# Four more third joins, six paired summing steps and a tenth read buffer in a one-core graph-network kernel

## The chip, the core and the metric

The kernel runs on one core of a Trainium2 chip. The metric is the device time of one execution in microseconds (us). Five engines work side by side: TensorE (PE; its weight loads are shown as PEld), VectorE (DVE), ScalarE (ACT), GpSimd (POOL) and SyncE (SP), which here only issues DMAs. They wait for each other through semaphores.

## What is computed

A graph layer over 6250 nodes and 206250 edges, padded to 1612 tiles of 128 edges:

```
msg  = concat(x[dst], edge_attr)             # per edge
h    = relu(msg @ W1a.T + b1a) @ W1b.T + b1b # per edge
agg  = segment_sum(h, src) / max(count, 1)   # per node
z    = relu(concat(x, agg) @ W2a.T + b2a) @ W2b.T + b2b
out  = layernorm(x + concat(z, x) @ Wr.T + br)
```

The second layer's weights are applied after the sum over the edges, so that only the first layer's rows, 128 wide, have to be summed per node. The edges come in the order of `dst`; the sum goes by `src`. The rows are therefore sorted through memory.

## The kernel before, in words

**Blocks.** The edges are taken in 124 blocks of 13 tiles. The loop runs `for k, ep_ in enumerate(epoch_of)`; PE, DVE, ACT and SP run in exactly the order in which the program is written (a manual schedule), GpSimd's queue holds the scatters.

**First layer and scatter.** For a block, `hidden` (matmuls at L1461, eviction with Relu by ACT at L1465) makes the first-layer rows of each tile in a row buffer `orow`; there are four (`ROWS`), so block k needs the buffer that block k-4 has scattered. `scatter` then sends each tile's 128 rows to their slots in the table `rows` in memory by one indirect DMA of GpSimd (L1513). The slots are sorted by `bin` = src // 128, of which there are 49. `scatter(k - LEAD)` is called two blocks behind.

**Joins.** In blocks 2 to 109 part of a block goes another way. A join takes three tiles and gathers edges of the same bin into quads of four rows. It costs marks (DVE at L1302, ACT at L1314 and L1318), six matmuls with the marks (L1348), a copy by ACT (L1353), eight matmuls for the rows (L1363) with two evictions (L1366), and one indirect DMA that scatters all quads (L1485). `joined(k)` says how many joins block k has: three in the blocks of the tuple `THRICE`, otherwise two. A block with j joins has 13 - 3j tiles that go directly, and so 13 - 2j scatters. The scatters of a block wait for places in the next block's work on PE (`pace`).

**Sums.** The rows of one bin are summed per node by one matmul for each tile of 128 slots (L1647, two matmuls each in the trace) against a one-hot matrix that DVE makes (L1627). The tiles come from memory by DMAs of SP (`read`, L1593) into the `READS` buffers `rt`. Low slots of a bin are full long before all edges are there: `FULL` lists, for each epoch, how many tiles a bin has when a step ends; `FULLQ` does so for the quads' slots. A step's reads wait until the scatters of the last blocks that may write there have landed. The first steps of both lists are paired: a group reads both steps' tiles of up to three bins, with at most 12 tiles (`SUMS, TILES = 3, 12`). A planner opens each pair three blocks (`LATE`) after its tiles are full, and gives each block as many tiles as `RATES[joined(k)]` allows. `sum_first`, `sum_rest` and `sum_next` do the sums; `collect` adds them to `part` (DVE at L1718; the first sum of a bin is copied by ACT). What is left when the joins end (10 tiles a bin) is summed from block 113 on. The blocks are three epochs of 110, 12 and 2 blocks with tables of their own: the second epoch's 162 tiles can be read when block 121 has been scattered, the last epoch's 51 when block 123 has.

**Other work in the loop.** Every second block from 10 to 58 computes two bins' share of the second layer ahead of time (`nodes_at`). `clear` has SP write zeros into slots that no edge may fill. `bins` splits src into bin and place (a few instructions of DVE and ACT) for blocks further on; src lies in memory that the read buffers `rt` use later (`lent`), so it has to be done before the first read.

**The end.** After the loop the last groups go through a pipeline of stages: means, product (POOL at L2056), transpose, second layer, residual, norm, store.

Of the kernel before, what the change touches and what calls it, by code (L numbers as in the profile page):

```python
# [453 lines left out]
NEAR = 8  # L454
HEAD = 117
NEXT = 468
FULL = ((3, 6, 9, 12), (1,), ())
BIG = 2.0**20
LATE = 3
RD = 6  # L460
SUMS, TILES = 3, 12
SEG = 9
PRE, AHEAD_FROM, EVERY = 9, 10, 2
RATES = {0: 55, 2: 18, 3: 10}
RING = 8
ROWS, EDGES, READS = 4, 4, 9
SPREAD = 4.8
EARLY = 30
CLEAR = 12
LEAD = 2  # L470
JOIN, QUAD, MARKS = 3, 4, 3
JOIN_FROM, JOIN_TO = 2, 110
THRICE = (*range(9, 27, 2), *range(34, 99, 8))
JOINS = 3 if THRICE else 2
PACED = range(PRE, 123)
SIDES, ENATS, CHUNK = 2, 2, 2
ON_ACT = 1
FULLQ = (3, 6, 9, 11, 13)
NODES = 8
FIRST = 4  # L480

# [8 lines left out]
def fast_path(  # L490
# [39 lines left out]
    NT = srcT.shape[1]  # L530
    E = NT * P
    NB = N // P + 1
# [22 lines left out]
    def joined(k):  # L555
        if not JOIN_FROM <= k < JOIN_TO:
            return 0
        return 3 if k in THRICE else 2

# [6 lines left out]
    def by_bin(of_bin, of_rest):  # L566
        return [of_bin] * (NB - 1) + [of_rest]
# [9 lines left out]
    def low_of(b, n, first=0):  # L577
        _, mean, dev = edges_of(b, n, first)
        return max(0, int(mean - dev)) // P
# [9 lines left out]
    def quads_low(b, n):  # L589
        _, mean, dev = quads_of(b, n)  # L590
        return max(0, int(mean - dev)) * QUAD // P
# [10 lines left out]
    for e, n in enumerate(EPOCHS):  # L602
# [15 lines left out]
        ep_.steps, lo = [], by_bin(0, 0)  # L618
        for t in FULL[e]:
            at = next(k for k in range(n) if low_of(0, k, ep_.first) >= t)  # L620
# [24 lines left out]
    qep.steps, lo = [], by_bin(0, 0)  # L645
    for t in FULLQ:
        at = next(k for k in range(qep.end + 1) if quads_low(0, k) >= t)
# [129 lines left out]
    with (  # L777
# [253 lines left out]

        NBAD = 15 + 5 * NE + 2 * sum(map(len, FULL)) + 2 * len(FULLQ)
        bad = const.tile([P, NBAD], F32, name="bad")
# [527 lines left out]
        def clear(e, i):  # L1561

            ep_ = epochs[e] if e else shared
            v = rows_of(ep_)
            step = (NB - 1) // CLEAR
            parts = [(i * step, (i + 1) * step)] + [(NB - 1, NB)] * (i == CLEAR - 1)
            for b0, b1 in parts:
                lo, hi_ = ep_.low[b0], max(ep_.top[b0:b1])
                if e:
                    lo, hi_ = ep_.stride // P - hi_, ep_.stride // P - lo  # L1570
                for l in range(lo, hi_, PADT):
                    c = min(l + PADT, hi_)
                    s = nc.sync.dma_start(
                        v[b0:b1, l * P : c * P, :].rearrange("b (p r) f -> p b (r f)", p=P),
                        padrow[:, None, : (c - l) * W].to_broadcast([P, b1 - b0, (c - l) * W]),
                    )
                    if e == 0:
                        for group_ in ("qslots", "slots0"):
                            tc.declare_no_dep(s.ins, group=group_, reason="no edge has these slots yet")
                        tc.add_to_no_dep_group("cleared", s.ins)  # L1580
                        cleared.append(s.ins)
# [71 lines left out]
        def groups_of(stage):  # L1653


            def size(b):
                return sum(st.hi[b] - st.lo[b] for st in stage)

            runs = []
            for b in range(NB):  # L1660
                if size(b) == 0:
                    continue
                if not runs or len(runs[-1]) == SUMS or sum(map(size, runs[-1])) + size(b) > TILES:
                    runs.append([])
                runs[-1].append(b)
            res = []
            for run in runs:
                reads = []
                for st in stage:
                    i = 0  # L1670
                    while i < len(run):
                        lo, hi_ = st.lo[run[i]], st.hi[run[i]]
                        nb, c = 1, hi_ - lo
                        while (
                            i + nb < len(run) and (st.lo[run[i + nb]], st.hi[run[i + nb]]) == (lo, hi_)
                            and (nb + 1) * c <= RD
                        ):
                            nb += 1
                        reads += [(st, run[i], nb, t0, n) for t0, n in tiles_of(lo, hi_)]
                        i += nb  # L1680
                res.append(reads)
            return res
# [69 lines left out]
        def tiles_in(groups):  # L1752
            return sum(nb * n for g in groups for _, _, nb, _, n in g)

        groups_at, queue, credit = [[] for _ in range(NGR + 1)], [], 0
        early_on = epochs[0].full
        assert len(early_on) <= len(qep.full)
# [6 lines left out]
        for k in range(NGR + 1):  # L1764
            for stage, at in zip(summing, open_at):
                if k == at:
                    queue += groups_of(stage)
            if k == NGR:
                groups_at[k] = queue
                break  # L1770
            until = min(o for o in opens if o > k)
            credit += min(RATES[joined(k)], max(tiles_in(queue) - credit, 0) / (until - k))
            while queue and credit > 0:
                groups_at[k].append(queue.pop(0))
                credit -= tiles_in(groups_at[k][-1:])
            credit = min(credit, 0)
        to_issue = []

        def issue(k):

            while to_issue and sum(len(g.reads) for g in issued + marked + halves) + len(to_issue[0]) <= READS:
                issued.append(Sums(k, to_issue.pop(0)))
# [17 lines left out]
        def nodes_cols(b0):  # L1800
            n = min(CHUNK, NB - b0)
            return n, slice(b0 * P, (b0 + n) * P)

        def nodes_load(b0):
            n, cols = nodes_cols(b0)
            have = min(N, cols.stop) - cols.start
            if have < n * P:
                nc.vector.memset(top.xin[:D, have : n * P], 0.0)
            nc.sync.dma_start(top.xin[:D, :have], xT[:, cols.start : cols.start + have])
# [18 lines left out]
                xrs[:, b0 : b0 + n, :], top.nx[:, n * P : n * (P + D)].rearrange("p (b f) -> p b f", f=D)  # L1828
            )

        nodes_at = {AHEAD_FROM + EVERY * i: b0 for i, b0 in enumerate(range(0, NB, CHUNK))}
        assert JOIN_FROM - 3 < AHEAD_FROM - 1 and max(nodes_at) < JOIN_TO

        bins_at = {NEAR - 2: (HEAD, NEXT), 22: (NEXT, 754), 24: (754, 1040), 26: (1040, 1326), 28: (1326, NT)}
        range_at = {4: (0, ALU.min), 5: (1, ALU.max)}
        assert NEXT % (SEG * BLK) == 0 and NEXT // BLK > max(bins_at) + 3
        for g in range(3):
# [9 lines left out]
        for k, ep_ in enumerate(epoch_of):  # L1847
# [71 lines left out]
            if k in range_at:  # L1919
                i, o = range_at[k]  # L1920
# [50 lines left out]
                nodes_store(nodes_at[k - 1])  # L1971
            if k + 1 in nodes_at:
                nodes_load(nodes_at[k + 1])
            if k in clears:
                clear(*clears[k])
            issue(k)

            if not joined(k):
                g = sum_first(k) if due > 0 else None
# [250 lines left out]
```

## Time and profile before

| | us |
|---|---|
| median of 3 runs | 1533.61 (1531.03 to 1533.70) |
| profiled execution | 1534.22 |
| its span, first to last instruction | 1532.4 |
| PE busy | 1440.7 (94%) |
| DVE busy | 1341.7 (88%) |
| POOL busy | 1128.8 (74%) |
| ACT busy | 1114.6 (73%) |

Mean granted TensorE clock over the span: 0.983. A busy share is a mean over stages with different limits; times on PE are modelled, so neighbouring matmuls overlap and the mean duration of one is longer than the distance between two starts. In rows of groups the numbers behind the bar are busy us, mean ns of one, and the engine's idle us before them with what ended it. In rows of the timeline stand the start, the length, engine, line, what is written and read, and in brackets the idle time before it. A row of a window has, for each engine, its busy us and its instructions in brackets; then the granted TensorE clock, the DMA share and GB/s.

### The profile page before, as it was taken

To read this page: it belongs to the slowest core of one execution; us is meant where nothing else is said; L and a number is where in the kernel's file an instruction comes from. 1 tells how busy PE (TensorE), PEld (TensorE's weight loads), DVE (VectorE), ACT (ScalarE), POOL (GpSimd) and SP (SyncE) were. 2 spreads that over 40 slices of the span, in tenths; PEclk is the share of its full clock that TensorE was granted. 3 is DMA by queue.
4 is the path that set the end of the run, shared out by engine and by line. 5 is a ranking of instruction groups with operands and counts; after the bars stand their busy time and mean duration, and the time that the engine had idled before them with its cause. 6 is when DMAs were issued, how large, how long until landed. Compare 5 with 4: busy or idle time off the path is not lost.

```text
span 1532.4 us, 33764 instructions
## 1 busy us (share of the span) xinstructions
PE 1440.7 (94%) x11008; PEld 1274.8 (83%) x11008; DVE 1341.7 (88%) x2882; ACT 1114.6 (73%) x2413; POOL 1128.8 (74%) x1198
## 2 busy tenths in 40 slices
PE   5989999987999999999989998999999999999997
PEld 4767777766888988888878888989888899999896
DVE  8789999887898988979889898999999988788787
ACT  3689999996898888878878887887887744332004
POOL 6777777777777777777777777777777777777734
PEclk9899999998999999999999999999999999999999
DMA  8798998967788888777877767777677899999884
GB/s 206 221 301 284 302 303 288 308 188 257 238 262 256 251 253 270 221 229 224 231 238 214 233 213 244 237 227 250 210 242 229 279 322 320 345 343 310 264 275 115
DMA packets 255427, 390.92 MB, mean 255 GB/s; under 512 B 43412, under 2 KB 186838, under 8 KB 255242
## 3 DMA queue, kind: packets, MB, share of 16 engines
q1 hardware_dynamic: 206874, 265.50, 58.7%
q0 software_dynamic: 47840, 122.94, 22.8%
q8 instruction: 90, 1.47, 0.4%
q14 instruction: 95, 0.78, 0.2%
q10 hardware_dynamic: 528, 0.22, 0.1%
HBM read 213.72 MB, written 174.78 MB: 254 GB/s over the span
## 4 chain that ended last, share of the span: by engine, by line
PE 57%; DMA 16%; ACT 11%; DVE 7%; issue 5%; POOL 2%; SPq 1%; DVEq 0%; ACTq 0%; POOLq 0%
PE place L1647 22%; PE place L1348 11%; DMA rows<-orow,rowidx 9%; PE place L1461 9%; PE place L1363 8%; DMA rt<-rows 3%; DMA rows<-orow,qidx 3%; ACT orow L1366 2%; ACT marks L1314 2%; ACT marks L1318 1%; DVE marks L1302 1%; POOL rows L1513 1%; DVE oh L1627 1%; ACT orow L1465 1%; ACT rhs L1414 1%
## 5 line engine op out<-in xcount | busy, mean ns | idle before, releaser
L1513 POOL DMA_INDIRECT rows<-orow,rowidx x910 | 878.3, 965 | 288.0 <-issue 142.5
L1647 PE MATMUL place<-rt,oh 128*128 128x129 f32 x3952 | 483.7, 277 | 15.3 <-ACT orow L1366 5.9
L1647 PEld LDWEIGHTS place<-rt,oh 128*128 128x128 f32 x3952 | 467.7, 193 | 27.2 <-DVE oh L1627 8.3
L1627 DVE TENSOR_TENSOR oh<-ramp,rt 128x768 f32<-128x768 bf16 (+4 forms) x391 | 309.6, 824 | 42.4 <-DMA rt<-rows 41.3
L1465 ACT ACTIVATE orow<-place 128x512 f32<-128x512 f32 (+2 forms) x263 | 142.5, 542 | 224.5 <-PE place L1461 219.3
L1485 POOL DMA_INDIRECT rows<-orow,qidx x234 | 226.1, 966 | 71.3 <-issue 19.8
L1302 DVE TENSOR_TENSOR marks<-quad_ramp,ramp 128x1024 fp32r<-128x1024 f32 x234 | 273.4, 1213 | 1.5 <-ACT z_act L1310 1.5
L1363 PE MATMUL place<-mv,rj 128*128 128x130 f32 x1872 | 242.7, 280 | 33.9 <-ACT orow L1465 20.6
L1348 PE MATMUL place<-marks,side 128*128 128x512 f32 x702 | 267.5, 410 | 0.0
L1461 PE MATMUL place<-mv,rhs 124*128 124x128 f32 x1820 | 262.5, 289 | 4.7 <-ACT orow L1465 3.8
L1363 PEld LDWEIGHTS place<-mv,rj 128*128 128x128 f32 x1872 | 223.1, 192 | 44.5 <-ACT orow L1465 24.5
L1348 PE MATMUL place<-marks,rest 128*64 128x512 f32 x702 | 240.2, 396 | 0.0
L1461 PEld LDWEIGHTS place<-mv,rhs 124*128 124x128 f32 x1820 | 229.6, 197 | 6.2 <-ACT orow L1465 4.0
L1348 PEld LDWEIGHTS place<-marks,side 128*128 128x128 f32 x702 | 134.3, 191 | 51.6 <-issue 2.0
L1366 ACT ACTIVATE orow<-place 128x260 f32<-128x260 f32 x468 | 163.7, 389 | 13.4 <-PE place L1363 4.1
L1314 ACT ACTIVATE marks<-quad_ramp,z_act 128x512 fp32r<-128x512 f32 x234 | 168.9, 722 | 6.1 <-PE place L1348 2.7
L1318 ACT ACTIVATE marks<-marks,ones 128x512 fp32r<-128x512 f32 x234 | 169.8, 725 | 4.1
L1121 DVE TENSOR_TENSOR_SCAN had<-ramp,bins 128x400 bf16<-128x400 bf16 (+2 forms) x124 | 127.2, 1026 | 13.7 <-ACT orow L1452 1.7
L1353 ACT COPY rj<-place 128x512 f32<-128x512 f32 x234 | 133.3, 570 | 1.9 <-PE place L1348 1.9
L1348 PEld LDWEIGHTS place<-marks,rest 128*64 128x64 f32 x702 | 96.0, 137 | 38.6 <-issue 0.8
L1414 ACT ACTIVATE rhs<-rhs,ones 60x896 f32<-60x896 f32 (+2 forms) x116 | 123.7, 1066 | 3.7
L1412 ACT ACTIVATE rhs<-rhs,from_win 60x896 f32<-60x896 bf16 (+2 forms) x116 | 123.6, 1065 | 2.9
(197 smaller groups left out, 1594.7 us busy)
## 6 DMA issues: line engine op xcount, KB each, us to landing
rt<-rows SPq DMA_DIRECT2D x194, 390.0 KB
rt<-rows SPq DMA_DIRECT2D x97, 325.0 KB
rows<-padrow SPq DMA_DIRECT2D x24, 1040.0 KB
rhs<-in_edgeT SPq DMA_DIRECT2D x90, 224.0 KB
enat<-in_edgeJ SPq DMA_DIRECT2D x90, 192.0 KB
rows<-orow,rowidx POOLq DMA_INDIRECT x910
rt<-rows SPq DMA_DIRECT2D x40, 260.0 KB
rt<-rows SPq DMA_DIRECT2D x48, 195.0 KB
```

The lines of the kernel that those rows point to most:

```text
L1302: nc.vector.tensor_tensor(m[:, :n, :], all_q[:, None, :].to_broadcast([P, n, QUAD * P]), z[:, :n, None].to_broadcast([P, n, QUAD * P]), op ...
L1314: nc.scalar.activation(m[:, t, :], all_q, AF.Square, bias=z_acts[k][:, i * JOIN + t : i * JOIN + t + 1], scale=-1.0)
L1318: nc.scalar.activation(m[:, t, :], m[:, t, :], AF.Relu, bias=ones[:, :1], scale=-1.0)
L1348: done[k, f"turn{i}"] = nc.tensor.matmul(ps[: w.shape[1], :], w, m[:, t, :], start=t + p == 0, stop=last and p == 1).ins.name
L1363: done[k, f"join{i}"] = nc.tensor.matmul(ps[:, j, :], rj[:, (g0 + j) * P : (g0 + j + 1) * P], m, start=True, stop=True).ins.name
L1366: nc.scalar.activation(mrow[:, g0 : g0 + 2, :], ps, AF.Relu)
L1461: done[k, c] = nc.tensor.matmul(ps[:, j, :], rhs[:WIDE, of * P : (of + 1) * P], m[:WIDE, :H], start=True, stop=True).ins.name
L1465: nc.scalar.activation(orow_of(k, k0, n)[:, :, :H], ps[:, :n, :], AF.Relu)
L1485: s = nc.gpsimd.indirect_dma_start(out=qep.rows.rearrange("(q r) f -> q (r f)", r=QUAD), out_offset=bass.IndirectOffsetOnAxis(ap=qidx[:, q ...
L1513: s = nc.gpsimd.indirect_dma_start(out=ep_.rows, out_offset=bass.IndirectOffsetOnAxis(ap=rowidx[:, k % RING * BLK + j : k % RING * BLK + j ...
L1627: nc.vector.tensor_tensor(res[:, at_tile : at_tile + nb * n, :], ramp[:, None, :].to_broadcast([P, nb * n, P]), node[:, :, None].to_broadc ...
L1647: m = nc.tensor.matmul(of_bin(b), oh[:, at, :], rows, start=i == 0, stop=i == len(of) - 1)
```

## The change

- `THRICE`: the blocks with three joins are, beside 9 to 25 in steps of 2, now 34 to 106 in steps of 6 (13 blocks) and no more 34 to 98 in steps of 8 (9 blocks): 22 for 18. There are 238 joins for 234.
- `FULL[0]` and `FULLQ` have six steps for four and five, all paired: 5, 4, 4, 4, 3 and 4 tiles a bin, where there were 6, 6, 6 and 5 tiles and a step of 2 tiles for the quads alone. A group can then hold three bins and not two. The first pair opens at block 28 (33 before). 11 tiles a bin stay for block 113 and later (10 before).
- `RATES[2]`: up to 14 tiles in a block with two joins (18 before), and `LESS`: 4 fewer in the blocks of `nodes_at`.
- `READS`: ten read buffers for nine.
- `bins_at`: the last four pieces of `bins` two blocks earlier.
- `issue(k)`, which issues reads, is called ahead of `clear` in a block.

```diff
-FULL = ((3, 6, 9, 12), (1,), ())
+FULL = ((2, 4, 6, 8, 9, 11), (1,), ())
...
-RATES = {0: 55, 2: 18, 3: 10}
+RATES = {0: 55, 2: 14, 3: 10}
+LESS = 4
 RING = 8
-ROWS, EDGES, READS = 4, 4, 9
+ROWS, EDGES, READS = 4, 4, 10
...
-THRICE = (*range(9, 27, 2), *range(34, 99, 8))
+THRICE = (*range(9, 27, 2), *range(34, 107, 6))
...
-FULLQ = (3, 6, 9, 11, 13)
+FULLQ = (3, 5, 7, 9, 11, 13)
...
+        nodes_at = {AHEAD_FROM + EVERY * i: b0 for i, b0 in enumerate(range(0, NB, CHUNK))}
...
-            credit += min(RATES[joined(k)], max(tiles_in(queue) - credit, 0) / (until - k))
+            credit += min(RATES[joined(k)] - LESS * (k in nodes_at), max(tiles_in(queue) - credit, 0) / (until - k))
...
-        nodes_at = {AHEAD_FROM + EVERY * i: b0 for i, b0 in enumerate(range(0, NB, CHUNK))}
...
-        bins_at = {NEAR - 2: (HEAD, NEXT), 22: (NEXT, 754), 24: (754, 1040), 26: (1040, 1326), 28: (1326, NT)}
+        bins_at = {NEAR - 2: (HEAD, NEXT), 20: (NEXT, 754), 22: (754, 1040), 24: (1040, 1326), 26: (1326, NT)}
...
                 nodes_load(nodes_at[k + 1])
+            issue(k)
             if k in clears:
                 clear(*clears[k])
-            issue(k)
```

## The prediction, written before the changed kernel ran

> **What bounds the kernel now.** I read the page first, then the windows, then GpSimd's timeline, last the chain and SP's waits around the end.
>
> ```profile
> span 1532.4 us, 33764 instructions
> PE 1440.7 (94%) x11008; PEld 1274.8 (83%) x11008; DVE 1341.7 (88%) x2882; ACT 1114.6 (73%) x2413; POOL 1128.8 (74%) x1198
> L1513 POOL DMA_INDIRECT rows<-orow,rowidx x910 | 878.3, 965 | 288.0 <-issue 142.5
> L1485 POOL DMA_INDIRECT rows<-orow,qidx x234 | 226.1, 966 | 71.3 <-issue 19.8
> ```
>
> By shares PE looks like the bound and POOL looks a quarter idle. Windows of single stages and POOL's own timeline say otherwise:
>
> ```profile
> 130.00:330.00 200.00, 190.68 (x1295) 152.48 (x1293) 186.39 (x436) 193.84 (x431) 151.39 (x158) 0.99 0.90 287
> 330.00:930.00 600.00, 564.78 (x4272) 496.89 (x4271) 520.73 (x1092) 503.26 (x1072) 456.40 (x472) 0.98 0.77 235
> 930.00:1230.00 300.00, 294.03 (x2332) 264.82 (x2331) 279.89 (x568) 241.06 (x495) 227.74 (x238) 1.00 0.77 242
> 1230.00:1400.00 170.00, 168.06 (x1485) 165.82 (x1484) 141.48 (x271) 64.06 (x86) 129.13 (x135) 1.00 1.03 334
> ...
> 77.63 0.96 POOL L1513 DMA_INDIRECT rows<-orow,rowidx  x1 [1.51 <-ACT orow L1366]
> 91.48 0.96 POOL L1513 DMA_INDIRECT rows<-orow,rowidx  x1 [2.54 <-ACT orow L1366]
> 262.53 0.96 POOL L1513 DMA_INDIRECT rows<-orow,rowidx  x1 [1.05 <-DMA rows<-orow,rowidx]
> ...
> 1380.08 0.96 POOL L1513 DMA_INDIRECT rows<-orow,rowidx  x1 [0.30 <-issue]
> 1381.34 0.95 POOL L1513 DMA_INDIRECT rows<-orow,rowidx  x1 [0.30 <-issue]
> ...
> 1467.27 0.96 POOL L1513 DMA_INDIRECT rows<-orow,rowidx  x1 [0.30 <-issue]
> ```
>
> In each window row the fifth busy time is POOL's, with its scatters in brackets: 158 in 200 us, 472 in 600, 238 in 300, 135 in 170. That is one per 1.26 to 1.27 us whatever PE does. The timeline shows why: 0.96 us busy, then 0.30 us that no wait explains, so starts lie 1.26 us apart (1380.08, 1381.34). After 20 us only three gaps are longer, 4.2 us together beyond their 0.30. So the 1144 scatters are one unbroken stream that ends at 1467.27 + 0.96 = 1468.23, and the "idle" 26% of POOL is a gap that comes with every scatter. POOL is the pacemaker of the blocks.
>
> PE runs ahead of it. The first block of 13 scatters, block 110, begins on PE at 1220.66 (first row below). On POOL 182 scatters remain from there: 1468.23 - 182 x 1.264 = 1238.2. The lead is 17.5 us. Four row buffers limit it: in the second row PE stands 4.20 us because a row buffer is not yet free.
>
> ```profile
> 1220.66 2.40 PE L1461 MATMUL place<-mv,rhs 124*128 124x128 f32 x20
> 923.95 0.71 PE L1363 MATMUL place<-mv,rj 128*128 128x130 f32 x4 [4.20 <-ACT orow L1465]
> ```
>
> The end matters as much, because 64 us follow the last scatter:
>
> ```profile
> SPq L1593 <- DMA rows<-orow,rowidx: 2.9, 2, 1.7
> ...
> 1438.36 5.39 DMA rt<-rows
> 1443.84 1.42 DVE L1627 TENSOR_TENSOR oh<-ramp,rt 128x768 f32<-128x768 bf16 x2 [1.22 <-DMA rt<-rows]
> 1444.86 11.21 PE L1647 MATMUL place<-rt,oh 128*128 128x129 f32 x98 [1.71 <-DVE oh L1627]
> 1444.00:1484.00 40.00, 38.51 (x336) 37.87 (x336) 35.32 (x65) 0.00 (x0) 18.41 (x20) 1.00 0.98 315
> ```
>
> The 162 tiles of the second epoch may be read only when the scatters of block 121 have landed. Its last scatter is the 27th from the end: 1467.27 - 26 x 1.264 + 0.96 = 1435.4. SP waits 2.9 us for that landing (first row, 1434 to 1445 us), issues at 1438.36, the data are there 5.39 us later, and PE, idle for 1.71 us, starts at 1444.86. From there PE works 38.51 of 40 us and the last stage follows. So this gate is tied to POOL's stream by 1444.86 - 1435.4 = 9.5 us, and everything behind it follows from it. PE reached the gate 1.71 us early, so in this kernel PE and POOL come out even.
>
> **The change, part by part.**
>
> 1. Four more third joins (22 for 18). A block with two joins issues 7 + 2 = 9 scatters, with three 4 + 3 = 7. POOL loses 4 x 2 = 8 scatters: 8 x 1.264 = 10.1 us, on the stream that has no idle time. The queue is not reordered. This is the only term that I put on the path in full.
>
> 2. What the third joins cost PE, per block:
>
> ```profile
> 991.79 1.85 PE place L1363 x16
> ...
> 1102.77 2.77 PE place L1348 x12
> 1112.76 2.77 PE place L1348 x12
> ...
> 1234.60 10.06 PE place L1647 x90
> 1245.25 2.23 PE place L1461 x20
> ...
> L1302 DVE TENSOR_TENSOR marks<-quad_ramp,ramp 128x1024 fp32r<-128x1024 f32 x234 | 273.4, 1213 | 1.5 <-ACT z_act L1310 1.5
> ```
>
> A join is 6 mark matmuls at 2.77/12 (1.39 us) and 8 row matmuls at 1.85/16 (0.93), less three first-layer tiles of two matmuls at 2.23/20 (0.67): +1.6 us, 6.5 us for four. This lies off POOL's path as long as PE keeps its lead. DVE makes two of the three marks of a join in 1.2 us (last row), 4.9 us for four; ACT makes the third. POOL's pace covers both (DVE is busy 520.73 of 600 us and 279.89 of 300, ACT less).
>
> 3. Summing steps. Both plans sum 1976 tiles (1925 before the last groups, worked out from the planner's lines), so PE's 3952 matmuls stay. Before, the paired steps took 6 tiles a bin and opened at block 33; 83 to 97 then got 24 and 12 tiles in turn. Now the sums open at block 28 with 10 tiles a block, then 12 (24 now and then), 9 and 18 near the end of the joined blocks, and 889 tiles are left from block 110 on, as before. Two-join blocks of 12 tiles last 9.99 us on PE (1102.77 to 1112.76); a tile costs 10.06/45 = 0.22. With 14 tiles that is 10.4 against POOL's 9 x 1.264 = 11.4; a three-join block with 10 takes 9.99 - 0.45 + 1.6 = 11.1 against 8.85. Six blocks: PE 63.3, POOL 65.7. PE gains 2.4 us in six blocks, so the lead is held by the buffers and not by work. As a check of the sum: in 330 to 1230 us PE is idle 900 - 564.78 - 294.03 = 41 us; less 10.1 and 6.5 leaves 24. I estimate a lead at block 110 of 22 to 27 us, where it was 17.5.
>
> 4. Groups of three bins for two: DVE adds 387 columns at a time. By the planner 75 adds of 258 and 17 of 387 become 85 of 387.
>
> ```profile
> L1718 DVE TENSOR_TENSOR part<-part,place 128x387 f32<-128x387 f32 x64 | 35.1, 549 | 2.1 <-PE place L1647 1.7 <-ACT sq L2089 0.3
> L1718 DVE TENSOR_TENSOR part<-part,place 128x258 f32<-128x258 f32 x72 | 29.1, 406 | 4.9 <-PE place L1647 4.7 <-ACT orow L1452 0.2
> ```
>
> 85 x 0.549 - 75 x 0.406 - 17 x 0.549 = +6.9 us over 900 us of DVE, hidden by POOL's pace (DVE idle: 79 of 600 us).
>
> 5. Reads. Most become 2 tiles a bin and not 3: shorter pieces, as many of them in all (389 reads become 392 by the planner). The DMA share in the stretch is 0.77, so nothing on the path. A tenth buffer allows five groups of two reads and not four: up to a group more ahead. Bound: nothing below, and 1.7 us gained at the gate if reads were what made PE wait there; they are held by the landing, so I take nothing.
>
> 6. The reads go ahead of the clears in SP's queue, and 4 chunks of bins move two blocks earlier, into the stretch where ACT is busy 193.84 of 200 us. That takes a little of PE's lead there. POOL's 158 scatters in that window show that the lead covers it; if the cover were gone, at most another gap like the one of 1.05 us at 262.53.
>
> 7. What comes new: PE would arrive at the gate 1.7 + 5 to 9 us early and stand idle for longer than the 4.20 us of the row shown above. Behind that wait came this:
>
> ```profile
> 917.00:924.80 7.80, 3.60 (x32) 3.34 (x31) 5.50 (x11) 4.00 (x11) 5.97 (x7) 1.00 0.89 304
> 924.80:928.20 3.40, 3.40 (x20) 3.12 (x20) 0.60 (x2) 2.86 (x5) 2.76 (x3) 0.50 0.13 43
> 928.20:936.00 7.80, 7.80 (x58) 6.83 (x59) 7.70 (x13) 4.50 (x10) 5.75 (x6) 1.00 0.65 159
> ```
>
> The granted clock (last but two) is 0.50 for 3.4 us after the wait. That costs half of 3.4 us, 1.7 us, and behind the gate PE is on the path. Bounds: 0 if PE idles less, 3.4 for two such stretches; I take 1.7, the row's case. The Trainium skill, page "TensorE: Matmul & The Clock Gate", section "Part 1: The HAM clock gate", speaks against the change here: after an idle window of about 3.4 us the clock is halved, and it takes a busy window of about that length to be released. The trace agrees (4.20 us idle, then 3.4 us at 0.50).
>
> Sum: -10.1 + 1.7 = -8.4 us. The profiled execution took 1534.22 us for a span of 1532.4; the median of the runs is 1533.61, 0.6 lower. 1533.6 - 8.4 = **1525.2 us**.
>
> **The rivals.**
>
> A. PE comes to the gate in time, but without the half clock: 1533.6 - 10.1 = 1523.5. Speaks for it: a lead at block 110 that grows by no more than 2 us. PE would then idle less than the 4.20 us.
>
> B. PE loses part of its lead. Each us by which the lead at block 110 falls below 17.5 takes one us of the 10.1 back. For it: PE at 294.03 of 300 us and DVE at 279.89 where the blocks were fullest, and the joins make them fuller. With a lead of 12 to 13: 1528.5.
>
> C. Slower: PE and no longer POOL sets the pace from block 34 on, with none of its idle time usable. PE's 6.5 us then come on top: 1533.6 + 6.5 = 1540. It decides from a lead of 7.4 us at block 110 (17.5 - 10.1) downwards; POOL would show gaps after "ACT orow". Against it: 41 us of PE idle in the stretch.
>
> D. The gate does not hold, because I read SP's 2.9 us wrongly, and PE's longer lead counts in full: some 8 us more (25 against 17.5): 1516. Against it: the 1.71 us of PE idle that the landing ends.
>
> E. Nothing moves: gaps of 0.30 us grow or new stalls eat the 8 scatters: 1533.
>
> **How the numbers follow.** Forecast 0.47, A 0.18, B 0.17, C 0.06, D 0.05, E 0.07. The range of 1520 to 1531 holds the forecast, A and B (0.82), with 1.7 us more below for a landing that comes sooner or a tenth buffer that helps. No change means within 0.2%, 3.1 us, about what a measurement of this kernel can tell. Faster: forecast, A, D and most of B, 0.86; same: E and the rest of B, 0.08; slower 0.06.
>
> **What would show it.** Right: 1136 scatters, still 1.26 us apart, the last one ending near 1458; no new gap over 1 us on POOL after block 28; PE's block 110 starting 22 us or more before POOL's; SP waiting for the landing of rows at some 1426 us for 8 us or so; PE idle before the second epoch's sums with a granted clock of 0.50 behind it; 49 us from block 121's last scatter to the last stage's first product on POOL, or 51 with the half clock. Wrong: gaps on POOL that PE or ACT end, a lead below 15 us at block 110, or an end that is not 97 to 99 us behind block 121's last scatter.

## The result and the profile after

| | before | changed |
|---|---|---|
| median, us | 1532.49 (4 runs, 1531.03 to 1533.70) | 1522.09 (4 runs, 1520.47 to 1524.90) |
| profiled execution, us | 1534.22 | 1524.90 |
| its span, us | 1532.4 | 1523.1 |

The ratio is 0.9931 [0.9915, 0.9947]: 10.4 us less by the medians, 9.3 by the spans of the two profiled executions. Line numbers are one higher in the changed kernel (the sums L1647 are now L1648, the scatters L1513 and L1485 now L1514 and L1486).

The head of the changed kernel's page and its two groups of scatters:

```profile
span 1523.1 us, 33850 instructions
PE 1439.5 (95%) x11048; PEld 1273.2 (84%) x11048; DVE 1355.1 (89%) x2926; ACT 1124.0 (74%) x2429; POOL 1125.0 (74%) x1190
L1514 POOL DMA_INDIRECT rows<-orow,rowidx x898 | 870.0, 969 | 283.2 <-issue 132.0
L1486 POOL DMA_INDIRECT rows<-orow,qidx x238 | 230.5, 969 | 72.5 <-issue 19.5
```

898 + 238 = 1136 scatters, eight fewer. Busy shares have hardly moved (PE 94 to 95%, POOL 74 to 74%); they would not tell that anything happened. GpSimd's timeline does, here the early gaps and the rows at block 110, block 121 and the end:

```profile
76.87 0.96 POOL L1514 DMA_INDIRECT rows<-orow,rowidx  x1 [0.80 <-ACT orow L1367]
85.99 0.96 POOL L1514 DMA_INDIRECT rows<-orow,rowidx  x1 [1.82 <-DVE hit_q L1232]
91.40 0.95 POOL L1514 DMA_INDIRECT rows<-orow,rowidx  x1 [1.92 <-ACT orow L1367]
...
1231.03 0.96 POOL L1514 DMA_INDIRECT rows<-orow,rowidx  x1 [0.30 <-DVE row L1261]
...
1427.03 0.96 POOL L1514 DMA_INDIRECT rows<-orow,rowidx  x1 [0.30 <-issue]
...
1459.91 0.96 POOL L1514 DMA_INDIRECT rows<-orow,rowidx  x1 [0.30 <-issue]
1474.99 0.83 POOL L2057 TENSOR_TENSOR agg<-part,rc 128x384 f32<-128x384 f32 x1 [14.11 <-issue]
```

After 91.40 us no gap is longer than 0.35 us: the stream is unbroken still and ends at 1460.87, 7.4 us earlier. PE's timeline and two windows of the blocks show what PE made of it:

```profile
1203.32 1.95 PE L1462 MATMUL place<-mv,rhs 124*128 124x128 f32 x16
...
1434.29 39.55 PE L1648 MATMUL place<-rt,oh 128*128 128x129 f32 x330 [9.34 <-DVE oh L1628]
330.00:930.00 600.00, 581.53 (x4491) 513.26 (x4490) 552.13 (x1169) 510.86 (x1088) 456.52 (x471) 1.00 0.82 243
930.00:1230.00 300.00, 293.47 (x2302) 262.26 (x2301) 281.60 (x607) 250.52 (x512) 228.08 (x237) 1.00 0.78 237
```

Block 110 starts on PE at 1203.32 and on POOL at 1231.03. The lead, by which PE starts a block ahead of POOL's first scatter of it, is 27.7 us; before, it was 18.0, from 1220.66 on PE and the first row below on POOL (the second row is used further down):

```profile
1238.66 0.96 POOL L1513 DMA_INDIRECT rows<-orow,rowidx  x1 [0.30 <-DVE part L1718]
...
1484.16 0.82 POOL L2056 TENSOR_TENSOR agg<-part,rc 128x384 f32<-128x384 f32 x1 [15.93 <-issue]
```

PE's idle time from 330 to 1230 us is 900 - 581.53 - 293.47 = 25.0 us. At the gate (the wait for block 121's rows ahead of the second epoch's sums) PE now stands for 9.34 us. SP's waits, the chain, DVE's timeline and two windows there:

```profile
SPq L1594 <- DMA rows<-orow,rowidx: 15.3, 6, 12.0
1429.58 3.60 DMA rt<-rows
1433.27 1.42 DVE L1628 TENSOR_TENSOR oh<-ramp,rt 128x768 f32<-128x768 bf16 x2 [8.85 <-DMA rt<-rows]
1428.80:1439.00 10.20, 4.71 (x22) 4.72 (x23) 4.94 (x9) 0.00 (x0) 7.76 (x9) 0.50 0.84 283
1439.00:1475.00 36.00, 35.77 (x316) 35.32 (x315) 30.53 (x57) 0.00 (x0) 16.70 (x19) 1.00 0.98 320
```

SP waits up to 12.0 us in one piece for block 121's rows, and the granted clock is 0.50 for 10.2 us. The span's 9.3 us divide at the gate so (before, after, difference):

```
last scatter of block 121 ends   1435.4   1427.99   -7.4
from there to the first sum         9.5      6.30   -3.2   (landing 1.4, first data 5.39 -> 3.60)
first sum to first POOL product   39.30     40.70   +1.4   (1484.16 and 1474.99)
from there to the end             48.2      48.1    -0.1
```

### The profile page after: what moved, and what is told of

It is laid out like the page before. It is cut to its first block, busy times and chain, and to the rows that moved or that the text cites. A ratio compares the mean times of both kernels' runs of the same rounds, so it can differ in the third digit from the quotient of the medians.

```text
span 1523.1 us, 33850 instructions
## 1 busy us (share of the span) xinstructions
PE 1439.5 (95%) x11048; PEld 1273.2 (84%) x11048; DVE 1355.1 (89%) x2926; ACT 1124.0 (74%) x2429; POOL 1125.0 (74%) x1190
## 4 chain that ended last, share of the span: by engine, by line
PE 63%; DMA 13%; ACT 9%; DVE 8%; issue 4%; POOL 2%; SPq 0%; DVEq 0%; ACTq 0%; POOLq 0%
PE place L1648 25%; PE place L1349 12%; PE place L1462 10%; PE place L1364 8%; DMA rows<-orow,rowidx 7%; DMA rows<-orow,qidx 4%; DVE marks L1303 2%; POOL rows L1514 2%; ACT marks L1315 2%; ACT orow L1367 1%; DVE oh L1628 1%; ACT marks L1319 1%; ACT rhs L1415 1%; ACT orow L1466 1%; PE cnt_ps L1164 1%
## 5 line engine op out<-in xcount | busy, mean ns | idle before, releaser
L1514 POOL DMA_INDIRECT rows<-orow,rowidx x898 | 870.0, 969 | 283.2 <-issue 132.0
L1648 PE MATMUL place<-rt,oh 128*128 128x129 f32 x3952 | 484.4, 276 | 27.9 <-DVE oh L1628 12.7
L1648 PEld LDWEIGHTS place<-rt,oh 128*128 128x128 f32 x3952 | 467.1, 192 | 42.7 <-DVE oh L1628 17.8
L1486 POOL DMA_INDIRECT rows<-orow,qidx x238 | 230.5, 969 | 72.5 <-issue 19.5
L1303 DVE TENSOR_TENSOR marks<-quad_ramp,ramp 128x1024 fp32r<-128x1024 f32 x238 | 277.7, 1211 | 2.0 <-ACT z_act L1311 2.0
L1349 PE MATMUL place<-marks,side 128*128 128x512 f32 x714 | 270.9, 409 | 0.0
L1462 PE MATMUL place<-mv,rhs 124*128 124x128 f32 x1796 | 256.9, 287 | 2.5 <-ACT orow L1466 1.7
L1364 PEld LDWEIGHTS place<-mv,rj 128*128 128x128 f32 x1904 | 224.5, 191 | 30.1 <-ACT rj L1354 17.8
L1349 PE MATMUL place<-marks,rest 128*64 128x512 f32 x714 | 243.7, 395 | 0.0
L1462 PEld LDWEIGHTS place<-mv,rhs 124*128 124x128 f32 x1796 | 224.5, 196 | 4.1 <-ACT orow L1466 1.9
L1466 ACT ACTIVATE orow<-place 128x384 f32<-128x384 f32 (+2 forms) x259 | 140.1, 543 | 117.3 <-PE place L1462 111.1
L1367 ACT ACTIVATE orow<-place 128x260 f32<-128x260 f32 x476 | 168.6, 389 | 18.0 <-PE place L1364 7.0
L1122 DVE TENSOR_TENSOR_SCAN had<-ramp,bins 128x400 bf16<-128x400 bf16 (+2 forms) x124 | 125.9, 1016 | 13.7 <-ACT orow L1453 1.1
```

Source lines behind the costliest of these rows:

```text
L1303: nc.vector.tensor_tensor(m[:, :n, :], all_q[:, None, :].to_broadcast([P, n, QUAD * P]), z[:, :n, None].to_broadcast([P, n, QUAD * P]), op ...
L1349: done[k, f"turn{i}"] = nc.tensor.matmul(ps[: w.shape[1], :], w, m[:, t, :], start=t + p == 0, stop=last and p == 1).ins.name
L1364: done[k, f"join{i}"] = nc.tensor.matmul(ps[:, j, :], rj[:, (g0 + j) * P : (g0 + j + 1) * P], m, start=True, stop=True).ins.name
L1367: nc.scalar.activation(mrow[:, g0 : g0 + 2, :], ps, AF.Relu)
L1462: done[k, c] = nc.tensor.matmul(ps[:, j, :], rhs[:WIDE, of * P : (of + 1) * P], m[:WIDE, :H], start=True, stop=True).ins.name
L1466: nc.scalar.activation(orow_of(k, k0, n)[:, :, :H], ps[:, :n, :], AF.Relu)
```

## The experiments

The theory: POOL's unbroken stream of scatters sets the pace, so 8 scatters are worth 8 x 1.264 us, if PE keeps its lead up to the gate; the new plan of sums is what keeps it. Rivals: the plan alone brings the time, or the tenth buffer and the order of reads; PE's work brings it down to less; the gate's clock.

**1 to 4, on another chip.** These were one part at a time: only the joins, all but the joins, nine buffers with the old order of reads, and a filled wait at the gate.

```diff
 e1_joins_only  (to the kernel before)
+THRICE = (*range(9, 27, 2), *range(34, 107, 6))
 e2_plan_only   (to the changed kernel)
+THRICE = (*range(9, 27, 2), *range(34, 99, 8))
 e3_nine_reads  (to the changed kernel; issue(k) behind clear again)
+ROWS, EDGES, READS = 4, 4, 9
 e4_warm_gate   (to the changed kernel, ahead of the second epoch's sums)
+                for _ in range(WARM):    # 32
+                    nc.tensor.matmul(ps, ident, ident, start=True, stop=True)
```

> The kernel before with the new THRICE alone (22 blocks with three joins; old steps, rates and nine buffers). Theory (POOL's scatters set the pace as long as PE keeps its lead): POOL loses 10.1 us, but behind block 84, where PE was already the tighter of the two, there are now four three-join blocks for two, each taking 1.6 + 2.5 = 4.1 us of lead. Lead at block 110: 17.5 - 8.2 = 9.3 us, so PE comes to the gate 8.2 - 1.7 = 6.5 us late: 10.1 - 6.5 = 3.6 us faster than before, about 1529. Rival 1 (fewer scatters are all that counts): 10 us faster. Rival 2 (PE is the bound, joins cost 6.5 us): 1539.

> The changed kernel with the old THRICE (18 blocks): the steps, rates, ten buffers and order of the change without its joins. Theory: POOL still has 1144 scatters, so the stream ends as before; at the gate the data come up to 3 us sooner because PE waits for them with empty queues, the half clock behind it takes 1.4 back: 0 to 2 us faster than before, 1531 to 1533, with a lead at block 110 of 25 us or more. Rival (the smoother plan makes the gain, the joins only add work): 10 us faster, 1522.

> The changed kernel with nine read buffers and with the reads issued behind the clears again. Theory: both lie under PE's lead, so within 1 us of the changed kernel, 1521 to 1523. Rival (the tenth buffer or the order feeds PE): 3 us or more of the gain is lost, 1525 or later, with more PE idle in front of the sums.

> The changed kernel with 32 matmuls more (128 x 128 of the identity, 0.22 us each, 7.2 us) on PE in front of the second epoch's sums, where PE idled 9.34 us and the clock then was 0.50 for 10.2 us. Their result is not used. Theory: the clock stays at 1.00 and the 330 matmuls behind the gate take 38.1 us as before and not 39.55: 1.4 us faster than the changed kernel, up to 2.4, about 1520.5. Rival (the half clock is hidden by reads that come no sooner): no difference, 1522.

On this chip the kernel before took 1905.82 us (median of 33), not 1532. Ratios: joins 1.0015 [0.9999, 1.0031], plan 1.0053 [1.0030, 1.0076], nine buffers 0.9994 [0.9978, 1.0011], filled gate 1.0023 [1.0003, 1.0044]. The third is the changed kernel but for its buffers and its order of reads, and it gains nothing here; the changed kernel itself was not run on this chip. The head of run 3's page, and two rows each of the waits of POOL and of PE:

```profile
span 1904.3 us, 33859 instructions
POOL rows L1514 <- issue: 213.2, 604, 2.3
POOL rows L1514 <- PE place L1349: 67.9, 54, 2.3
...
PE place L1364 <- issue: 84.5, 50, 4.6
PE place L1648 <- issue: 54.6, 88, 3.0
```

On the first chip the changed kernel's PE has one such row, 1.2 us in 2 pauses; here PE stands 84.5 us in 50 pauses of up to 4.6 us with nothing shown that it waits for, and POOL waits for PE in pieces of 2.3 us. POOL is not the pacemaker there, and by the theory saved scatters then bring nothing: none of the four kernels was faster. The times that I had expected assumed the other case, so these runs could not test the theory; what stalls that chip is open. All that follows ran on one other chip, where the kernel before takes 1530 to 1532 us (its median over 25 runs beside runs 5 to 8: 1531.41; over 10 runs beside 9 to 12: 1530.48).

**5. More third joins: every fourth block.**

```diff
-THRICE = (*range(9, 27, 2), *range(34, 107, 6))
+THRICE = (*range(9, 27, 2), *range(34, 107, 4))
```

> The changed kernel with three joins in every fourth block from 34 to 106 (28 such blocks for 22). Theory: POOL has 12 scatters fewer, 15.2 us; PE needs 6 x 1.6 = 9.6 us more, and four blocks take it 3 x 10.4 + 11.1 = 42.3 us against POOL's 43.0, so it just keeps its lead: 12 to 15 us faster than the changed kernel where POOL's scatters stand 1.26 us apart, about 1508. Rival (PE is the bound by now): no gain or 5 to 10 us slower, with gaps on POOL that PE or ACT end. If this chip again has issue stalls of 1 to 4 us on PE, ACT and DVE, POOL is not the pacemaker and the ratio to the kernel before stays within 0.5% of 1.

1535.78, ratio 1.0028 [1.0012, 1.0045]: slower, with 12 scatters fewer than the changed kernel. My forecast (about 1508) failed and the rival, PE as the bound, held. Two places of POOL's timeline, then PE's rows for block 110 and the gate:

```profile
607.69 0.96 POOL L1514 DMA_INDIRECT rows<-orow,rowidx  x1 [2.01 <-PE place L1648]
609.75 0.96 POOL L1514 DMA_INDIRECT rows<-orow,rowidx  x1 [1.10 <-ACT orow L1367]
...
829.28 0.96 POOL L1514 DMA_INDIRECT rows<-orow,rowidx  x1 [0.98 <-PE place L1648]
831.35 0.96 POOL L1514 DMA_INDIRECT rows<-orow,rowidx  x1 [1.10 <-ACT orow L1367]
...
1218.86 1.39 PE L1462 MATMUL place<-mv,rhs 124*128 124x128 f32 x11
...
1444.91 37.13 PE L1648 MATMUL place<-rt,oh 128*128 128x129 f32 x330 [0.40 <-DVE oh L1628]
```

The gaps are ended by PE and by the eviction behind it; after block 28 they hold 20.2 us beyond 0.30 each. The lead is down to 6.5 to 13 us from block 60 on, and at the gate PE idles 0.40 us where the changed kernel idles 9.34: PE starts these sums at 1444.9, as before, and SP's waits there no longer list the landing of block 121's rows. Two stretches of four blocks take PE 43.0 and 44.6 us (starts at 840.22, 883.17, 927.75); POOL needs 34 x 1.264 = 43.0. By my price of a join it would have been 42.3. The denser joins also push sums back: from its start of block 110 to the gate PE makes 1526 matmuls of L1648, and 1478 in the changed kernel, 24 tiles or some 5 us more.

**6 and 7. One part at a time again**, with the edits of 1 and 2.

> The kernel before with the new THRICE alone, once more, since in the first series every kernel, that before included, took 1900 us and POOL was not the pacemaker. Theory, where POOL's scatters stand 1.26 us apart: lead at block 110 of 9.3 us, 3.6 us faster than before. Rival 1 (scatters are all that counts): 10 us faster. Rival 2 (PE is the bound): 6 us slower.

> The changed kernel with the old THRICE, once more for the same reason. Theory, where POOL's scatters stand 1.26 us apart: 0 to 2 us faster than before, lead at block 110 of 25 us or more. Rival (the plan makes the gain): 10 us faster.

Joins alone: 1535.65, 1.0027 [1.0009, 1.0045], 4 us slower, where I expected 3.6 faster (the lead came out as expected, 10.9 us for 9.3). Plan alone: 1530.69, 0.9992 [0.9976, 1.0007], no change. Together they bring 10 us. POOL's timeline of the joins alone shows its only two long gaps after block 28 and the stream's end; PE's shows block 110 and the gate; the last row is the gate in the plan alone:

```profile
1210.07 0.96 POOL L1513 DMA_INDIRECT rows<-orow,rowidx  x1 [2.37 <-PE cnt_ps L1164]
1230.63 0.96 POOL L1513 DMA_INDIRECT rows<-orow,rowidx  x1 [1.89 <-DMA rt<-rows]
...
1460.90 0.96 POOL L1513 DMA_INDIRECT rows<-orow,rowidx  x1 [0.30 <-issue]
1221.04 1.73 PE L1461 MATMUL place<-mv,rhs 124*128 124x128 f32 x14
...
1448.06 37.44 PE L1647 MATMUL place<-rt,oh 128*128 128x129 f32 x330 [0.39 <-DVE oh L1627]
...
1441.41 38.67 PE L1648 MATMUL place<-rt,oh 128*128 128x129 f32 x330 [6.58 <-DVE oh L1628]
```

With the joins alone the stream does end 6.4 us earlier (1461.86; 3.4 of it because block 28 began earlier in that execution), but PE idles only 0.39 us at the gate and starts the second epoch's sums at 1448.06, 3.2 us later than before: PE is the bound there, and POOL's saving is lost behind it. With the plan alone PE stands 6.58 us at the gate, waiting for an unshortened stream. The lead in us, from the starts of the blocks on PE and POOL, shows which part does what:

| block | before | joins alone | plan alone | changed |
|---|---|---|---|---|
| 81 | 30.2 | 29.9 | 30.1 | 27.9 |
| 93 | 21.4 | 21.1 | 25.9 | 26.9 |
| 106 | 17.4 | 8.5 | 26.3 | 23.7 |
| 110 | 18.0 | 10.9 | 29.9 | 27.7 |

At block 81 they lie within 2.3 us of each other. In single blocks before it they differ by up to 12 us, but the means over blocks 28 to 81 are alike: 26.6, 26.8, 24.9 and 24.1 us in the order of the columns. Then the old plan, with 24 and 12 tiles in turn, lets the lead fall by 12 us, and the joins take 7 more; the means over blocks 100 to 110 are 18.2, 13.7, 27.5 and 25.4. The new plan has done more of the work by then: in the changed kernel PE makes 4491 matmuls from 330 to 930 us and not 4272, and its idle time there falls from 35 to 18 us. The plan is several edits (steps, rates, the earlier `bins`, buffers, order of reads); run 11 clears the last two, and the others were not tried apart.

**8. The wait at the gate filled**, edit as in 4: 32 identity matmuls.

> The changed kernel with 32 matmuls of the identity (7.2 us of PE) in front of the second epoch's sums, their result not used, once more for the same reason. Theory: clock 1.00 behind the gate, the 330 matmuls there take 38.1 us and not 39.55, 1.4 us faster than the changed kernel (11 to 12 faster than before). Rival: no difference to the changed kernel (10 faster than before).

1520.34, 0.9918 [0.9898, 0.9938], the lowest ratio of all. PE's timeline of it, one window and POOL's first product; then the same window and the first sum in the changed kernel's second profile (run 9):

```profile
1421.10 7.31 PE L2036 MATMUL place<-ident 128*128 128x128 f32 x64
1430.27 11.21 PE L1649 MATMUL place<-rt,oh 128*128 128x129 f32 x98 [1.85 <-DVE oh L1629]
1426.30:1436.50 10.20, 8.35 (x74) 8.15 (x74) 6.55 (x12) 0.00 (x0) 7.67 (x8) 1.00 1.01 346
...
1469.09 0.82 POOL L2063 TENSOR_TENSOR agg<-part,rc 128x384 f32<-128x384 f32 x1 [12.55 <-issue]
```

```profile
1430.35 40.68 PE L1648 MATMUL place<-rt,oh 128*128 128x129 f32 x330 [8.96 <-DVE oh L1628]
1426.30:1436.50 10.20, 6.15 (x28) 6.15 (x29) 7.16 (x13) 0.00 (x0) 7.76 (x9) 0.50 0.98 328
```

With the wait filled the granted clock stays at 1.00 and 74 matmuls are done where 28 were (some of the 74 are the filling). The first sum starts at the same time, 1430.27 and 1430.35, and the first POOL product follows it by 1469.09 - 1430.27 = 38.8 us, not 1472.18 - 1430.35 = 41.8: the half clock cost 3.0 us in that execution, and 40.70 - 38.82 = 1.9 in the first profile. That idling brings it on is shown. By the medians it is 0.6 to 2.6 us (1520.92 and 0.9935 for run 9), and the intervals overlap: the direction agrees, the size is not settled by times. The ten traces of before, changed and runs 5 to 12 settle it better. In us: PE's idle time at the gate, the time from block 121's last scatter to the first sum, the part of the half clock that lies behind the first sum, and from there to the first POOL product:

| profile | PE idle at the gate | last scatter to first sum | half clock behind it | first sum to product |
|---|---|---|---|---|
| before | 1.71 | 9.5 | 0 | 39.3 |
| 5 | 0.40 | 18.0 | 0 | 38.3 |
| 6 | 0.39 | 19.1 | 0 | 38.6 |
| 8, wait filled | 1.85 | 6.6 | 0 | 38.8 |
| 7 | 6.58 | 6.3 | 3.2 | 39.8 |
| 11 | 4.60 | 6.4 | 3.3 | 39.8 |
| 12 | 3.37 | 6.1 | 3.4 | 39.9 |
| changed | 9.34 | 6.3 | 4.8 | 40.7 |
| 10 | 3.69 | 6.5 | 5.6 | 41.0 |
| 9 | 8.96 | 6.3 | 6.2 | 41.8 |

The last column grows with the half clock, from 38.3 to 39.3 us without it to 41.8 at 6.2 us of it. So it costs 1 to 3 us, and how much does not follow the length of the wait before it. The Trainium skill, "TensorE: Matmul & The Clock Gate", section "Part 1: The HAM clock gate", says "The warm-up budget is ~3.4 µs of time, not a number of matmuls." The trace is of that order, without one fixed figure: of the 10.2 us at half clock PE was still waiting in some 5.5 in the first profile and 4.1 in the second, and with PE at work again at the gate the clock came back after 3.2 to 6.2 us (the fourth column; 4.5 us in run 12, where the half clock began 1.1 us behind the first sum).

**9 to 11. The changed kernel again, with more work for PE, and with nine buffers.**

```diff
 e10_more_pe  (in each block from 28 to 109)
+                ps = hp.take(P)
+                nc.tensor.matmul(ps, ident, ident, start=True, stop=True)
+                hp.leave(ps)
 e11_nine_reads_again: as e3
```

> The changed kernel as it is, beside the next three on one chip, so that they can be held against it. All theories: 0.993 of the kernel before, 1521 to 1523, if POOL's scatters stand 1.26 us apart; with issue stalls on PE, ACT and DVE as in the first series, within 0.3% of the kernel before.

> The changed kernel with one more matmul (128 x 128 of the identity, 0.22 us, result not used) in each block from 28 to 109: 82 x 0.22 = 18.3 us more work on PE. Theory (POOL is the pacemaker, PE's lead is the buffer): the lead at block 110 falls from 27.7 to about 16 us, the end moves by 0 to 2 us, 1522 to 1524, and POOL shows no gap. Rival (PE, 63% of the chain, is the bound): 18 us slower, 1540.

> The changed kernel with nine read buffers and the reads behind the clears, once more where POOL sets the pace. Theory: within 1 us of the changed kernel. Rival (the tenth buffer or the order feeds PE): 3 us or more slower than it.

1520.92 (0.9935 [0.9920, 0.9949]), 1520.91 (0.9937 [0.9923, 0.9951]) and 1521.20 (0.9936 [0.9920, 0.9952]): one time for all three. The group of the added matmuls and the two windows in the second:

```profile
L1978 PE MATMUL place<-ident 128*128 128x128 f32 x164 | 37.8, 312 | 0.0
330.00:930.00 600.00, 590.60 (x4595) 524.00 (x4594) 551.79 (x1169) 509.77 (x1087) 456.46 (x472) 1.00 0.81 244
930.00:1230.00 300.00, 297.55 (x2346) 267.04 (x2345) 280.55 (x604) 250.29 (x512) 228.10 (x236) 1.00 0.76 235
```

PE is busy 13.1 us longer in the 900 us, at 590.60 of 600, and the time does not move; the lead at block 110 falls to 23.35 (I expected some 16). This is the plainest evidence that PE, the "95% busy" engine, does not set the pace of the changed kernel, and that the lead at block 110 is spare down to some value between 11 (runs 5 and 6: too little) and 18 (before). Run 12's lead went down to 15.4 in single blocks without a gap on POOL. The tenth buffer and the order of reads are worth no time that can be measured: with nine buffers PE idles 4.60 us at the gate and not 9, so it does come later, but still ahead of the data. Runs 7 and 9 have the same plan and differ by the four joins alone, that is by eight scatters: from block 28's first scatter on the stream is 9.6 us shorter (1145.6 and 1136.0 us) and the median 9.8 us lower (1530.69 and 1520.92; 8.7 us by their ratios to the kernel before).

**12. Every fifth block.**

```diff
-THRICE = (*range(9, 27, 2), *range(34, 107, 6))
+THRICE = (*range(9, 27, 2), *range(34, 107, 5))
```

> The changed kernel with three joins in every fifth block from 34 to 104 (24 such blocks for 22). Theory, with a third join at 2.4 us of PE and not 1.6 as the runs so far show: POOL has 4 scatters fewer, 5.1 us; five blocks take PE some 55 us against 54.3, so the lead falls by 0.7 us in five blocks, to 15 to 18 us at block 110, and PE comes to the gate even with POOL: 3 to 5 us faster than the changed kernel, 1517 to 1519. Rival (the lead is lost as with every fourth block): as slow as the kernel before, 1530, with gaps on POOL.

1520.71, 0.9932 [0.9918, 0.9946]: not the 3 to 5 us less than the changed kernel that I expected, but 0.2. The lead did not fall to 15 to 18 us at block 110 either, it is 22.7, and PE is still 3.37 us early at the gate. Its PE, POOL and ACT timelines at the gate and the end, then the same of run 9:

```profile
1429.41 38.77 PE L1648 MATMUL place<-rt,oh 128*128 128x129 f32 x330 [3.37 <-DVE oh L1628]
1469.33 0.83 POOL L2057 TENSOR_TENSOR agg<-part,rc 128x384 f32<-128x384 f32 x1 [13.14 <-issue]
1511.19 0.27 ACTq L2114 DMA_DIRECT2D out_dram<-y  x1
```

```profile
1472.18 0.83 POOL L2057 TENSOR_TENSOR agg<-part,rc 128x384 f32<-128x384 f32 x1 [15.22 <-issue]
1514.04 0.27 ACTq L2114 DMA_DIRECT2D out_dram<-y  x1
```

From block 28's first scatter to the last one's end its stream is 4.2 us shorter than run 9's (1131.9 and 1136.0), and block 28 began 3.4 us later: the gaps between 75 and 93 us, before any of this, come to 0 to 4.7 us in the different executions. The last store still goes out 2.85 us sooner (4.2 of stream and 1.9 of half clock, less the 3.4, make 2.7), but the span ends 9.2 us behind it, not 5.8 (1520.4 - 1511.19 and 1519.8 - 1514.04). So in this pair of executions the saving is there at the last store and is given back in its landing. Run 5 showed the same long landing (8.7 us), the other profiles 5.7 to 6.6. Why these two kernels store slower at the end, and whether each of their executions does, was not tried and stays open.

## Why the prediction was right, point by point

Forecast 1525.2, measured 1522.09; the forecast case occurred: PE early at the gate, with the half clock behind it. The mechanism held; that the number came so close is in part luck. In the profiled spans the stream gave 2.7 us less than the 10.1 forecast, and a step that I had left unchanged gave 3.2 us that I had not counted.

- **Eight scatters, -10.1.** Right in kind. From block 28's first scatter to the end of the last, the stream took 1144.75 us before, 1137.20 in the changed kernel's first profile, 1136.04 in its second and 1134.03 in run 8: 7.6 to 10.7 less. The rest of the spread is the scatter itself: 969 ns in the first profile, 965 before (967.7 and 964.5 with the quads' scatters, from block 28 on: 2.9 us over 894), 965 in run 8. The last one ended at 1460.87 and 1456.95, around the 1458 foretold.
- **A third join, +1.6 us of PE.** Too low. In the changed kernel blocks 63 and 64 take 15.90 + 6.50 us for 24 tiles (starts below), two blocks with 24 tiles and two joins each 2 x 9.99: 2.4 us, of which 1.1 was idle before the join. My sum of instructions left the wait out.

```profile
686.87 0.54 PE L1462 MATMUL place<-mv,rhs 124*128 124x128 f32 x3
702.77 0.36 PE L1462 MATMUL place<-mv,rhs 124*128 124x128 f32 x1
709.27 0.56 PE L1462 MATMUL place<-mv,rhs 124*128 124x128 f32 x3
752.15 0.54 PE L1462 MATMUL place<-mv,rhs 124*128 124x128 f32 x3
```

- **The lead, 22 to 27 us.** It was 27.7, near the range, but not for my reason, so the figure was luck. I had PE gain 2.4 us on POOL in six blocks (63.3 to 65.7); blocks 63 to 68 took it 65.28 (752.15 - 686.87), a gain of 0.4. The lead is there because the even plan keeps it from falling between blocks 81 and 110 (table of runs 6 and 7). My second count, 24 us of PE idle left of 41, met the 25.0 measured, though the same window now holds work of later blocks.
- **DVE's wider adds, reads, the tenth buffer, the order of issue: 0.** Confirmed by run 11 for the last two; DVE was busy 552.13 of 600 us (520.73 before, since more sums fall into this stretch), and POOL shows no gap behind it.
- **The half clock, +1.7.** 1.4 against before by the product behind the gate, 1.9 to 3.0 against the filled gate of run 8. It lasted 10.2 us and not 3.4, but PE was still waiting for reads in some half of them. The row of 3.4 us that I took was not the only case in that profile: from 378.6 us the clock was 0.50 for 6.8 us, around a wait of 4.02.
- **What the sum lacked.** The step from block 121's last scatter to the first sum shrank from 9.5 to 6.3 us. I had kept it at 9.5. 1.4 of it is the landing (SP issues 1.59 us behind the scatter's end, before 2.96), 1.8 the first data (3.60 for 5.39). The step is 6.1 to 6.6 us in every profile in which PE comes clearly early (table of run 8), with 18 third joins (run 7) as with 22, so it goes with PE's early arrival and not with the eight scatters. PE had then used up the earlier reads; that the empty queue of reads is the cause is argued, not shown. My markers "49 or 51 us to the first POOL product" and "97 to 99 to the end" came out as 47.0 and 95.1 for this reason; an end outside the 97 to 99 was one of the signs of being wrong that I had named, and it was this step that was wrong, not POOL's stream. Without it the span would have been 1526.3, without the half clock 1521.7.
- **Rivals.** Rival A's 1523.5 lies nearer to the measured time than the forecast does. The time can't tell the two apart; the lead of 27.7 us and the clock of 0.50 do. E is excluded by the ratio, 0.9915 to 0.9947. B's rule, one us lost for each us of lead below 17.5, was wrong as a rule. For the joins alone, with a lead of 10.9, it gave 1531.5 - 10.1 + 6.6 = 1528.0, and 1535.65 was measured. It missed that the joins alone leave 20 tiles more behind block 110, 20 x 0.22 = 4.4 us more for PE ahead of the gate: in the traces PE makes 1534 matmuls of L1647 from its start of block 110 to the gate, and 1494 before. C, PE as the bound, is what runs 5 and 6 are; in the changed kernel run 10 excludes it. D (the gate does not hold) is excluded by SP's wait of 12.0 us.

## What to carry to other kernels

An engine that shows a quarter of its time as idle can be the pacemaker: look for a gap that comes with every instruction and that no wait explains (here 0.96 us busy and 0.30 us of nothing, 1136 times). What a shorter stream on it is worth is decided by the other engine's lead at the gates, which the starts of the same block on both engines give directly; here the shorter stream alone cost 4 us, the better-spread work alone brought nothing, and both together brought 10. When a gain seems to vanish, follow it to the last instruction: in the one profiled pair of run 12 it was there at the last store and lost in its landing.

## What was not expected of the hardware

- The same kernel took 1906 us on one chip and 1531 on another. On the first, run 3's profile has pauses of up to 4.6 us on PE that no wait explains, and kernels near the changed one gained nothing there; the changed one gained 10 us on the other.
- The half clock came in stretches of 3.4, 6.8 and 10.2 us, and their length does not follow the wait: 3.4 us after an idle of 4.20 and 6.8 after 4.02 in the profile before; at the gate 3.4 after 4.60 (run 11), 6.8 after 3.69 (run 10) and after 6.58 (run 7), 10.2 after 9 in two profiles.
- From the issue of the last store to the end of the span it took 5.7 to 6.6 us in eight profiles and 8.7 and 9.2 in two (runs 5 and 12); the mean of one direct scatter (L1514) was 964 to 969 ns from execution to execution, which over 1136 of them is several us.
